# Rows of x by indexed gathers on GpSimd in place of plain loads on ScalarE's queue

## The chip, the cores and the metric

The kernel runs on one NeuronCore of one Trainium2 chip. The metric is the device time of one execution in microseconds (us). Engines are called PE (TensorE, with PEld for its weight loads), DVE (VectorE), ACT (ScalarE), POOL (GpSimd) and SP (SyncE). ACTq and SPq are the sequencers of ACT and SP, which issue transfers. L235 is line 235 of a kernel. All runs quoted are fast, which here means that none was more than 1.5% above the fastest of its kernel. The granted clock is the share of its full clock that PE was allowed.

A ratio below is the mean time of one kernel's fast runs over the mean of the other's fast runs in the same rounds, so it isn't quite the ratio of the medians that are quoted beside it. Brackets behind a ratio are its 95% interval.

## The reference, cut to what matters

Four graph layers over 2708 nodes with 512 features each follow one another, each with a residual and a layer norm. All of them multiply by the same 2708 x 2708 adjacency. Layer 0, and the counts that layer 1 needs, are:

```python
adj_hat = adj + eye(N)
d = 1.0 / sqrt(adj_hat.sum(axis=1))
x = layernorm(x + (d[:, None] * adj_hat * d[None, :] @ x) @ W.T + b)   # layer 0
mask = adj > 0           # layer 1 divides by roots of the row counts of this mask
# layers 1 to 3: further products with adj, attention, binarized weights (left out)
```

## The kernel before

The change touches the first stage only. It goes over 22 blocks of 128 rows (the last has 20). For each block it loads the rows of x and a row tile of the adjacency, computes x times W0 on PE, sums the adjacency rows on ACT, counts their non-zeros on DVE, and takes the power -1/2 of each sum on GpSimd. Layer 0 can start its first product when all blocks of `fc` are there.

```python
nc.scalar.dma_start(b0_row, over_partitions(b0, D))    # then bg_row, ba_col, bb_col, all on ACT's queue
...
weights(w0, w0_t)                                      # 1 MB, on ACT's queue too
for b in range(NB):
    m = rows(b)
    nc.scalar.dma_start(fb[b][:m], x[b * P : b * P + m, :])                 # L235
    ar = pre.tile([P, N], F32, tag="arow", name=f"arow{b}", bufs=2)         # two buffers
    nc.sync.dma_start(ar[:m], adj[b * P : b * P + m, :])                    # L237, 1.39 MB
    xt = transposed(pre, fb[b], b, F32, ident, "xt0_")                      # PE (L187), copied by ACT (L189)
    ps = project(xt, b, w0, "y0_")                                          # PE, 8 products for two blocks (L196)
    nc.scalar.activation(ar[:m], ar[:m], AF.Copy, accum_out=row_sum[:m, b : b + 1])   # L240, the "sum"
    nc.vector.tensor_scalar(ar[:m], ar[:m], 0.0, 0.0, op0=ALU.is_gt, op1=ALU.add,
                            accum_out=row_cnt[:m, b : b + 1])               # L241, the "count"
    dc = dinv[:m, b : b + 1]
    nc.vector.tensor_scalar(dc, row_sum[:m, b : b + 1], 1.0, None, op0=ALU.add)
    nc.gpsimd.tensor_tensor(dc, dc, neg_half[:m], op=ALU.pow)               # L247
    nc.vector.tensor_scalar(fc[b][:m], ps[:m], dc, None, op0=ALU.mult)      # L248
    nc.vector.tensor_tensor(fb[b][:m], fb[b][:m], b0_row[:m], op=ALU.add)   # L249, the bias add
```

SP's queue also carries chunks of the transposed adjacency for layer 0, seven of them in the first 64 us. A scheduler orders the instructions of each engine, and one that waits holds up those behind it: in the kernel before, ACT had summed adjacency tile 0 by 12.2 us, but DVE's count of it, behind a bias add that waited for x until 21.97 us, started at 22.57. An edit to one line can move the others.

Of the kernel before, what the change touches and what calls it, by code (L numbers as in the profile page):

```python
# [12 lines left out]
PSUM = bass.MemoryType.PSUM  # L13

P = 128
# [5 lines left out]


def over_partitions(row: bass.AP, n: int):
    """A contiguous row of n elements in DRAM, read once per partition."""
    return bass.AP(tensor=row.tensor, offset=row.offset, ap=[[0, P], [1, n]])


# [1 line left out]
def kernel(  # L29
# [15 lines left out]
    w3_t: bass.AP,  # L45
    out: bass.AP,
):
    """Four residual graph layers with layer norm.

    Every product with the adjacency takes 128 x 128 tiles of its transpose (contraction index on  # L50
    the partitions) as the stationary operand and 128 x 512 node features as the moving one. The
    features stay in SBUF in three buffers of one tile per 128 nodes; the transposed adjacency, which
    doesn't fit beside them, is streamed in column groups, ahead of the products.
    """
    nc = tc.nc
    N, D = x.shape
    KC = D // P
    NB = -(-N // P)
    W = 2 * P
# [3 lines left out]
    AHEAD = 6  # L63
    PREP = 2
# [7 lines left out]
    def blocks(g: int):  # L72
        return [b for b in (2 * g, 2 * g + 1) if b < NB]

    # The contraction tiles of one column group, in chunks of one load each: (first tile, tiles, rows).
    parts = [(j, min(CH, NFULL - j), P) for j in range(0, NFULL, CH)]
    if N % P:
        parts.append((NFULL, 1, N % P))
# [5 lines left out]
    stream = ctx.enter_context(tc.tile_pool(name="stream", bufs=AHEAD + 1))  # L84
# [5 lines left out]
    fa = [feat.tile([P, D], F32, tag=f"fa{b}", name=f"fa{b}") for b in range(NB)]  # L90
    fb = [feat.tile([P, D], F32, tag=f"fb{b}", name=f"fb{b}") for b in range(NB)]
    fc = [feat.tile([P, D], F32, tag=f"fc{b}", name=f"fc{b}") for b in range(NB)]
# [5 lines left out]
    ones = const.tile([P, 1], F32, name="ones")  # L98
# [11 lines left out]
    bb_col = const.tile([P, 1], F32, name="bb_col")  # L110
    nc.scalar.dma_start(bb_col, over_partitions(bb, 1))

    # Per node, node b * 128 + p at [p, b]; the rows that the last block lacks stay 1.
    row_sum = const.tile([P, NB], F32, name="row_sum")
    row_cnt = const.tile([P, NB], F32, name="row_cnt")
    dinv = const.tile([P, NB], F32, name="dinv")
    head = const.tile([P, NB], F32, name="head")
    rdeg = const.tile([P, NB], F32, name="rdeg")
    nc.vector.memset(row_sum, 1.0)
    nc.vector.memset(row_cnt, 1.0)  # L120
    # x3 columns: x.Wa[:D], x.Wa[D:], x.Wb[:D], x.Wb[D:], h.a[:D], h.a[D:]
    cols = const.tile([P, NB, 6], F32, name="cols")
    nc.vector.memset(cols, 1.0)

# [1 line left out]
    chunk_of = {}  # L126
    issued = [0]

# [14 lines left out]
            issued[0] += 1  # L143

    def run_layer(layer: int, products, prep, finish):
        """products names a block's PSUM accumulators; prep(g, part, adj) gives, for each of them, what
        a chunk's products read: (stationary chunk, moving tiles); finish(b, *accumulators) ends a
        block. prep runs PREP chunks ahead of the products, the loads AHEAD."""
        base = layer * PER_LAYER
        ready = {}  # L150
        acc = {}
        for k in range(PER_LAYER):
            for q in range(k, min(k + PREP, PER_LAYER - 1) + 1):
                if q not in ready:
                    load_until(base + q + (AHEAD - PREP))
                    ready[q] = prep(*divmod(q, NPART), chunk_of.pop(base + q))
            g, part = divmod(k, NPART)
            operands = ready.pop(k)
            if part == 0:
                acc = {  # L160
                    b: [ps_mm.tile([P, D], F32, tag="mm", name=f"l{layer}_{n}_{b}") for n in products]
                    for b in blocks(g)
                }
            j0, nj, r = parts[part]
            for jj in range(nj):
                j = j0 + jj
                for ib, b in enumerate(blocks(g)):
                    m = rows(b)
                    for ps, (lhs, rhs) in zip(acc[b], operands):
                        nc.tensor.matmul(  # L170
                            ps[:m, :],
                            lhs[:r, jj, ib * P : ib * P + m],
                            rhs[j][:r, :],
                            start=(j == 0),
                            stop=(j == NB - 1),
                        )
            if part == NPART - 1:
                for b in blocks(g):
                    finish(b, *acc[b])

# [1 line left out]
    def transposed(pool, src, b: int, dt, eye, name: str):  # L182
        """Rows of block b with the features on the partitions: [128, D / 128, rows]."""
        m = rows(b)
        ps = ps_sm.tile([P, KC, P], dt, tag="sm", name=f"{name}p{b}")
        for k in range(KC):
            nc.tensor.transpose(ps[:, k, :m], src[:m, k * P : (k + 1) * P], eye[:m, :m])  # L187
        t = pool.tile([P, KC, P], dt, tag=name, name=f"{name}{b}", bufs=2)
        nc.scalar.copy(t[:, :, :m], ps[:, :, :m])  # L189
        return t  # L190
# [8 lines left out]
        return ps  # L199

    def as_row(dst, src, name: str):
        """dst[:, i] = the value of node i on every partition; src(b) is block b's column."""
        for b0_ in range(0, NB, KC):
            ps = ps_sm.tile([P, KC * P], F32, tag="sm", name=f"{name}{b0_}")
            n = 0
            for b in range(b0_, min(b0_ + KC, NB)):
                m = rows(b)
                nc.tensor.transpose(
                    ps[:, n : n + m], src(b)[:m].to_broadcast([m, P]), ident[:m, :m]
                )  # L210
                n += m
            nc.scalar.copy(dst[:, b0_ * P : b0_ * P + n], ps[:, :n])
# [13 lines left out]
    def weights(dst, src):  # L226
        nc.scalar.dma_start(dst, src.rearrange("(k p) o -> p k o", p=P))

# [1 line left out]
    with tc.tile_pool(name="pre0", bufs=1) as pre:  # L230
        w0 = pre.tile([P, KC, D], F32, name="w0")
        weights(w0, w0_t)
        for b in range(NB):
            m = rows(b)
            nc.scalar.dma_start(fb[b][:m], x[b * P : b * P + m, :])  # L235
            ar = pre.tile([P, N], F32, tag="arow", name=f"arow{b}", bufs=2)
            nc.sync.dma_start(ar[:m], adj[b * P : b * P + m, :])  # L237
            xt = transposed(pre, fb[b], b, F32, ident, "xt0_")
            ps = project(xt, b, w0, "y0_")
            nc.scalar.activation(ar[:m], ar[:m], AF.Copy, accum_out=row_sum[:m, b : b + 1])  # L240
            nc.vector.tensor_scalar(  # L241
                ar[:m], ar[:m], 0.0, 0.0, op0=ALU.is_gt, op1=ALU.add,
                accum_out=row_cnt[:m, b : b + 1],
# [5 lines that stand above are left out]
            nc.vector.tensor_tensor(fb[b][:m], fb[b][:m], b0_row[:m], op=ALU.add)  # L249
        nc.gpsimd.tensor_tensor(head, row_cnt, half, op=ALU.pow)  # L250
        nc.vector.tensor_scalar(head, head, HEAD_EPS, None, op0=ALU.max)
        nc.vector.reciprocal(head, head)
        nc.vector.tensor_tensor(rdeg, row_cnt, head, op=ALU.mult)
        nc.vector.tensor_tensor(rdeg, rdeg, row_sum, op=ALU.add)
        nc.vector.reciprocal(rdeg, rdeg)

# [1 line left out]
    def finish0(b, ps):  # L258
        m = rows(b)
        t = work.tile([P, D], F32, tag="t", name=f"t0_{b}")  # L260
# [5 lines left out]

    run_layer(0, ["y"], lambda g, part, a: [(a, fc)], finish0)

# [1 line left out]
    with tc.tile_pool(name="l1", bufs=1) as l1:  # L270
        head_row = l1.tile([P, N], F32, name="head_row")
        as_row(head_row, lambda b: head[:, b : b + 1], "head_")
# [20 lines left out]

        run_layer(1, ["e"], prep1, finish1)

# [1 line left out]
    with tc.tile_pool(name="l2", bufs=1) as l2:  # L297
        sl_row = l2.tile([P, N], F32, name="sl_row")
        with tc.tile_pool(name="pre2", bufs=1) as pre:
# [34 lines left out]
            nc.vector.tensor_scalar(cols[:, :, 1], cols[:, :, 1], ba_col, None, op0=ALU.add)  # L334
            nc.vector.tensor_scalar(cols[:, :, 3], cols[:, :, 3], bb_col, None, op0=ALU.add)

# [1 line left out]
        # The attention's columns of adj, and sum e, are summed over the contraction tiles on  # L338
        # VectorE and GpSimd, and over the partitions by one product with ones for each block.
        with tc.tile_pool(name="main2", bufs=2) as main:  # L340
            sums = {}

# [65 lines left out]

            run_layer(2, ["b", "a"], prep2, finish2)

# [1 line left out]
    with tc.tile_pool(name="pre3", bufs=1) as pre:  # L412
        w3 = pre.tile([P, KC, D], F32, name="w3")
        weights(w3, w3_t)
# [9 lines left out]
            ps = project(xt, b, bw, "xw_")  # L424
            nc.vector.tensor_copy(fc[b][:m], ps[:m])

# [1 line left out]
    def finish3(b, ps):  # L428
        m = rows(b)
        t = work.tile([P, D], F32, tag="t", name=f"t3_{b}")  # L430
# [50 lines left out]
```

## Time and profile before

| | before |
|---|---|
| median of 2 runs | 2584.46 us (2584.16 to 2584.76) |
| PE busy before layer 0's first product, 0 to 152.6 us | 102.86 us |
| PE busy in layer 0, 152.6 to 584 us | 429.22 of 431.40 us |
| ACT's sum of adjacency tile 6 starts | 63.53 us |
| ACT's sum of adjacency tile 20 starts | 144.64 us |
| issues of x on ACT's queue | 22, median 0.416 us |

Where PE is full (429.22 of 431.40 us), nothing that the change does can matter. The first 152.6 us are read by three landmarks: the sum of tile 6 (end of a disturbed start), the sum of tile 20 (end of a regular loop), and layer 0's first product. The group of the x loads shows why they are worth a look at all. Its first line gives count, shortest, median and longest issue in ns, and the start of the first and last. Below it stands who waited for them, in us and times:

```profile
L235 ACTq DMA_DIRECT2D fb<-in_x_dram x22: 334/416/621, 3.6 to 64.0; - x22
...
who waited for it (us, times):
  PE xt_p L187: 20.8, 1
```

PE waited once, 20.8 us, for the first of them.

### The profile page before, as it was taken

Reading aid. Unit: us, or ns where it says so; the run is one execution under the profiler, and the core shown is the slowest. Engines: PE = TensorE matmul, PEld = TensorE weight load, DVE = VectorE, ACT = ScalarE, POOL = GpSimd, SP = SyncE. Lnnn points to the kernel's source line nnn. Section 1 sums busy time; section 2 is a strip of 40 time slices with the busy share of each in tenths; the row PEclk is TensorE's granted clock in tenths of the full one; section 3 lists DMA queues with packets and bytes.
Section 4 is the critical chain, followed back from the end, with each engine's and each line's share of the span. In section 5 each row is a group of like instructions: output and inputs, shape, how many; then the busy total and the mean of one; then the engine's idle time right before and its main releaser. Section 6 shows DMA issues by size and latency. Waiting matters only on the chain.

```text
span 2585.0 us, 16339 instructions
## 1 busy us (share of the span) xinstructions
PE 2486.2 (96%) x6073; PEld 1065.1 (41%) x6073; DVE 996.6 (39%) x1771; ACT 342.0 (13%) x560; POOL 273.5 (11%) x359
## 2 busy tenths in 40 slices
PE   5799999999999998999999999999999989999998
PEld 2334444424444442444444444444444324444442
DVE  4731110115444542001866656676656332011011
ACT  3510000000000000111323222232212211000000
POOL 0010000000000000000322212222222100000000
PEclk9899999999999998999999999999999989999999
DMA  8632222222222222000111111111111011223220
GB/s 320 225 106 68 72 76 69 68 61 80 71 71 80 68 54 73 0 1 0 31 31 37 31 43 32 34 35 37 37 32 26 23 47 52 81 85 90 82 83 27
DMA packets 136625, 164.07 MB, mean 63 GB/s; under 512 B 6822, under 2 KB 125990, under 8 KB 133838
## 3 DMA queue, kind: packets, MB, share of 16 engines
q1 hardware_dynamic: 127574, 146.69, 19.9%
q10 hardware_dynamic: 8972, 16.35, 1.8%
q8 instruction: 47, 0.77, 0.1%
q14 instruction: 32, 0.26, 0.0%
HBM read 157.46 MB, written 5.55 MB: 63 GB/s over the span
## 4 chain that ended last, share of the span: by engine, by line
PE 94%; DMA 3%; DVE 1%; ACT 1%; issue 1%; ACTq 0%; POOL 0%; POOLq 0%; DVEq 0%
PE l_b L170 17%; PE l_e L170 17%; PE l_a L170 16%; PE l_o L170 16%; PE l_y L170 16%; PE h L196 3%; PE g L196 3%; PE y L196 2%; DMA arow<-in_adj_dram 1%; DMA fb<-in_x_dram 1%; PE xw L196 1%; ACT xt L189 1%; PE xt_p L187 1%; PE ps L386 1%; PE pc L327 1%
## 5 line engine op out<-in xcount | busy, mean ns | idle before, releaser
L170 PE MATMUL l_b<-fc,adj 128*128 128x512 f32 x968 | 511.1, 610 | 0.0
L170 PE MATMUL l_a<-fa,e 128*128 128x512 f32 x968 | 504.3, 604 | 0.0
L170 PE MATMUL l_e<-fa,inc 128*128 128x512 f32 x968 | 427.8, 599 | 2.1 <-DVE inc L283 2.1
L170 PE MATMUL l_y<-fc,adj 128*128 128x512 f32 x968 | 426.1, 597 | 0.0
L170 PE MATMUL l_o<-fc,adj 128*128 128x512 f32 x968 | 426.1, 597 | 0.0
L170 PEld LDWEIGHTS l_a<-fa,e 128*128 128x128 f32 x968 | 183.8, 190 | 244.0 <-issue 239.9
L170 PEld LDWEIGHTS l_b<-fc,adj 128*128 128x128 f32 x968 | 178.6, 190 | 246.7 <-issue 244.7
L170 PEld LDWEIGHTS l_e<-fa,inc 128*128 128x128 f32 x968 | 175.1, 186 | 254.0 <-issue 243.4
L170 PEld LDWEIGHTS l_y<-fc,adj 128*128 128x128 f32 x968 | 174.5, 185 | 251.5 <-issue 243.8
L170 PEld LDWEIGHTS l_o<-fc,adj 128*128 128x128 f32 x968 | 174.5, 185 | 251.1 <-issue 244.3
L374 POOL TENSOR_TENSOR sum_e<-sum_e,e 128x256 f32<-128x256 f32 (+2 forms) x231 | 186.3, 806 | 470.6 <-ACT e L364 458.5
L221 POOL TENSOR_TENSOR rs<-rs,neg_half 128x1 f32<-128x1 f32 x88 | 64.1, 729 | 1378.0 <-DVE rs L220 1242.5
L376 DVE SCALAR_TENSOR_TENSOR sum_a<-adj,cols,sum_a 128x256 f32<-128x256 f32 (+2 forms) x231 | 141.3, 612 | 44.8 <-DMA adj<-in_adj_t_dram 44.8
L431 DVE SCALAR_TENSOR_TENSOR t<-l_o,fb 128x512 f32<-128x512 f32 (+1 forms) x22 | 15.0, 682 | 370.5 <-PE l_o L170 370.5
L280 DVE SCALAR_TENSOR_TENSOR inc<-adj,head_row 128x768 f32<-128x768 f32 (+1 forms) x88 | 75.3, 857 | 213.0 <-PE l_e L170 212.3
L376 DVE SCALAR_TENSOR_TENSOR sum_b<-adj,cols,sum_b 128x256 f32<-128x256 f32 (+2 forms) x231 | 152.2, 659 | 0.0
L261 DVE TENSOR_TENSOR t<-l_y,fc 128x512 f32<-128x512 f32 (+1 forms) x22 | 15.1, 687 | 350.1 <-PE l_y L170 350.1
L364 ACT ACTIVATE e<-e 128x768 f32<-128x768 f32 (+1 forms) x88 | 67.5, 767 | 528.0 <-DVE e L363 527.7
L362 DVE TENSOR_SCALAR e<-adj 128x768 f32<-128x768 f32 (+1 forms) x88 | 46.3, 526 | 229.9 <-PE l_a L170 229.7
L196 PE MATMUL y<-w,xt 128*128 128x512 f32 (+1 forms) x176 | 92.7, 686 | 28.9 <-ACT xt L189 28.9
L189 ACT COPY xt<-xt_p 128x512 f32<-128x512 f32 (+1 forms) x66 | 35.4, 566 | 566.2 <-PE xt_p L187 558.2
L355 ACT ACTIVATE z<-sl_row,cols 128x256 f32<-128x256 f32 (+1 forms) x242 | 103.0, 485 | 0.0
(94 smaller groups left out, 1268.6 us busy)
## 6 DMA issues: line engine op xcount, KB each, us to landing
adj<-in_adj_t_dram SPq DMA_DIRECT2D x280, 384.0 KB
arow<-in_adj_dram SPq DMA_DIRECT2D x21, 1354.0 KB
adj<-in_adj_t_dram SPq DMA_DIRECT2D x28, 222.0 KB
fb<-in_x_dram ACTq DMA_DIRECT2D x21, 256.0 KB
out_dram<-o ACTq DMA_DIRECT2D x21, 256.0 KB
w<-in_w_t_dram ACTq DMA_DIRECT2D x2, 1024.0 KB
wsa<-in_w_sa_dram ACTq DMA_DIRECT2D x1, 1024.0 KB
wg<-in_w_gcnb_dram ACTq DMA_DIRECT2D x1, 1024.0 KB
```

The lines of the kernel that those rows point to most:

```text
L170: nc.tensor.matmul(ps[:m, :], lhs[:r, jj, ib * P : ib * P + m], rhs[j][:r, :], start=(j == 0), stop=(j == NB - 1),)
L187: nc.tensor.transpose(ps[:, k, :m], src[:m, k * P : (k + 1) * P], eye[:m, :m])
L189: nc.scalar.copy(t[:, :, :m], ps[:, :, :m])
L196: nc.tensor.matmul(ps[:m, :], xt[:, k, :m], weight[:, k, :], start=(k == 0), stop=(k == KC - 1))
L221: nc.gpsimd.tensor_tensor(rs[:m], rs[:m], neg_half[:m], op=ALU.pow)
L280: nc.vector.scalar_tensor_tensor(inc[:r, :nj, :w], av, 0.0, row, op0=ALU.is_gt, op1=ALU.mult)
L327: nc.tensor.matmul(pc[:m, :6], xt[:, k, :m], vec[:, :, k], start=(k == 0), stop=(k == KC - 1))
L355: nc.scalar.activation(z[:r, jj, :w], sl_row[:r, g * W : g * W + w], AF.Identity, bias=cols[:r, j0 + jj, 5:6],)
L362: nc.vector.tensor_scalar(ev, av, 0.0, MASKED, op0=ALU.is_equal, op1=ALU.mult)
L364: nc.scalar.activation(ev, ev, AF.Exp, scale=-1.0)
L374: nc.gpsimd.tensor_tensor(se[:r, :w], se[:r, :w], ej, op=ALU.add)
L376: nc.vector.scalar_tensor_tensor(s[:r, :w], aj, u, s[:r, :w], op0=ALU.mult, op1=ALU.add)
```

## The change

Its intent is to take 22 load issues off ACT, which also does the sums and the copies. GpSimd was busy for 12.98 of the first 152.6 us. A column of row numbers is made once, and each block of x is fetched by an indexed gather whose indices are just its own row numbers. The diff also blanks comments and docstrings, which is cut here:

```diff
@@ -226,13 +226,20 @@
     with tc.tile_pool(name="pre0", bufs=1) as pre:
+        node = pre.tile([P, NB], mybir.dt.int32, name="node")
+        nc.gpsimd.iota(node, pattern=[[P, NB]], base=0, channel_multiplier=1)
         w0 = pre.tile([P, KC, D], F32, name="w0")
         weights(w0, w0_t)
         for b in range(NB):
             m = rows(b)
-            nc.scalar.dma_start(fb[b][:m], x[b * P : b * P + m, :])
+            nc.gpsimd.indirect_dma_start(
+                out=fb[b][:m],
+                out_offset=None,
+                in_=x,
+                in_offset=bass.IndirectOffsetOnAxis(ap=node[:m, b : b + 1], axis=0),
+            )
```

## The prediction

> **What bounds the kernel now.** I read the page first, then the execution cut into its stages, then the chain of waits of the first stage in order of time, then that stage's timeline.
>
> The page's chain that ended last says that nearly all of the span is TensorE:
>
> ```profile
> PE 94%; DMA 3%; DVE 1%; ACT 1%; issue 1%; ACTq 0%; POOL 0%; POOLq 0%; DVEq 0%
> PE l_b L170 17%; PE l_e L170 17%; PE l_a L170 16%; PE l_o L170 16%; PE l_y L170 16%; PE h L196 3%; PE g L196 3%; PE y L196 2%; DMA arow<-in_adj_dram 1%; DMA fb<-in_x_dram 1%; PE xw L196 1%; ACT xt L189 1%; PE xt_p L187 1%; PE ps L386 1%; PE pc L327 1%
> ```
>
> The change touches only "DMA fb<-in_x_dram 1%". The execution by stage (columns: stretch in us, its length, busy us of PE, weight loads, DVE, ACT, POOL with counts, granted clock, DMA share, GB/s):
>
> ```profile
> 0.00:152.60 152.60, 102.86 (x265) 46.92 (x265) 94.18 (x114) 67.74 (x67) 12.98 (x27) 0.92 0.71 257
> 152.60:584.00 431.40, 429.22 (x991) 176.84 (x990) 63.81 (x141) 2.92 (x6) 15.88 (x23) 1.00 0.25 68
> ```
>
> From 152.6 us on PE is full (429.22 of 431.40), and no x is read any more. So the change can act on the first 152.6 us alone, 6% of 2584.46. There no engine is full; DMA share is 0.71. The chain of waits of that stage (start us, us, what):
>
> ```profile
> 3.58 17.13 DMA fb<-in_x_dram
> 20.84 1.10 PE xt_p L187 x4
> ...
> 113.12 8.83 PE y L196 x16
> 121.95 0.89 PE xt_p L187 x8
> 122.87 0.90 issue
> 123.77 0.20 ACT arow L240
> 123.99 2.98 DVE arow L241 x2
> 126.97 0.03 DVE dinv L246
> 127.00 6.16 DMA arow<-in_adj_dram
> ```
>
> Two regimes. At the start everything waits for the first x tile, which lands at 20.7 us. From about 60 us on it is a loop: DVE counts an adjacency row tile (2.98), its buffer (one of two) comes free, the next tile is loaded (6.16; others 5.6 to 5.7), ACT sums it (2.46 + 0.19), DVE counts it. 5.7 + 2.65 + 2.97, plus small gaps, makes about 11.4 us for a buffer, two tiles. The trace agrees: ACT's sum of tile 6 starts at 63.53, of tile 20 at 144.64, 14 tiles in 81.1 us, 5.79 us each. The x tiles were all asked for by 64.05 us and are not in that loop.
>
> The start in the timeline:
>
> ```profile
> 12.04 0.19 ACT L240 ACTIVATION_READ_ACCUMULATOR arow<-arow 128x1 f32 x1
> ...
> 21.97 0.69 DVE L249 TENSOR_TENSOR fb<-fb,b_row 128x512 f32<-128x512 f32 x1 [20.40 <-PE xt_p L187]
> ...
> 22.57 2.96 DVE L241 TENSOR_SCALAR_CACHE_REDUCE arow<-arow 128x2708 f32<-128x2708 f32 x1
> ...
> 25.58 3.29 SPq L237 DMA_DIRECT2D arow<-in_adj_dram  x2
> ```
>
> Tile 0 was summed at 12.2 us, but its count on DVE stands behind the bias add of x tile 0, so it started at 22.57, and the third adjacency load was issued only at 25.58. DMA is loose there: 170 GB/s from 20 to 25 us against 344 to 404 from 30 to 50.
>
> [...] the early stretches at 344 to 404 GB/s look like a shared limit. [...] ACT's issues took 334 to 621 ns (median 416) here; the trace has no gather. [...]
>
> **The change part by part.** I compared the built orders of both kernels.
>
> *Removed from ACT*: 22 issues of about 0.42 us, 9.2 us in all. ACT is busy 67.74 of 152.6 us and waits 59.8 us for adjacency tiles, so this alone is worth nothing; what matters is that ACT's later x loads stood behind its sums and copies.
>
> *Added on GpSimd*: one iota (128 x 22) and 22 gathers. Before, GpSimd is busy 12.98 us here. [...] Eight semaphores serve the gathers, so the ninth and later ones each wait for the landing of the one eight before. GpSimd also computes the powers that release DVE's scaling of each block, and in the new order the power of block 2 stands behind gather 19 and that of block 3 behind gather 21, the last. After that GpSimd is as before.
>
> *Moved on DVE and SP*: the count of adjacency tile 0 now comes before the first bias add. It can start when ACT has summed tile 0: 12.2 us before, perhaps 13 now as three queues share the start. Then the third adjacency load goes out near 16 us in place of 25.6, 9 us earlier.
>
> *How much of the 9 us is kept.* The early stage then runs into DMA. Before the sum of tile 6 can start, 7 tiles of 1.39 MB (9.7 MB), 7 transposed chunks of 0.39 MB (2.75), W0 and two bias rows (1.57) and most of x (14 to 22 tiles of 0.26, 3.7 to 5.8 MB) must move: 17.7 to 19.8 MB. Before, about 20 MB had moved by 63.5 us (296, 296 and 347 GB/s over three 20 us stretches, then 361). With fewer holes at 340 to 360 GB/s from 2.5 us on, that is 52 to 60 us; I take 57.5, so 6 us gained.
>
> *The loop* has the same cycle; only the pairing of blocks shifts by one (0-1, 2-3 in place of 0, 1-2, 3-4). From tile 6 on I expect 5.7 to 5.8 us a tile, no gain.
>
> *The tail*: before, block 21 stood alone after the sum of tile 20, and its product started at 147.36, 1.9 us of PE idle, then layer 0 at 152.6. Now blocks 20 and 21 are a pair ahead of the sum of tile 20, so layer 0 may start about 2 us sooner.
>
> Sum: 6 + 2 = 8 us. 2584.5 - 8 = 2576.5; I say 2577.
>
> **Rivals.** (1) *GpSimd becomes the gate.* If a gather holds it for g us, the power of block 3 comes at about 2 + 22g us. The count of tile 4 comes some 3 us after it (scalings 2 x 0.75, two bias adds 1.3), and it started at 51.97 before. So it equals the kernel before at g = (51.97 - 5)/22 = 2.1 us; each further us costs 22. At g = 3 the kernel takes about 20 us more, 2604; over 2% slower (52 us) needs g of about 4.5. For it: in-order GpSimd, and no measured gather. [...] The same gate through landings: gather 21 waits for gather 13, which at a quarter to a third of 350 GB/s lands near 35 to 45 us. That fits, but narrowly.
> (2) *x pushes ahead of adjacency.* Up to eight gathers in flight, 2.1 MB, are 6 us at 350 GB/s; if they only delay tiles 0 to 3 and leave no hole filled, the gain is gone: 2584 to 2588.
> (3) *The first x was the whole trouble*: without that wait all 9 to 10 us plus the tail are kept, 2572.
> (4) *Hidden anyway*: 2584.
>
> **Range and chances.** Rivals 2 to 4 lie between 2572 and 2588, a slow gather of up to 2.4 us adds about 6 to the upper end. I take 2566 to 2591. To be 2% faster the first stage would have to shrink from 152.6 to 101 us, under its 102.86 us of PE work: 1%. 2% slower needs gathers over 4 us each: 2%. Within: 97%.
>
> **What would show it.** Right: DVE's first count near 13 to 16 us, the third adjacency load before 18, layer 0's first product near 145, and every later stage within 1 us. ACT's sum of tile 6 near 57 shows the DMA step; 5.7 to 5.8 us a tile after it shows the loop unchanged. Wrong: DVE's scalings waiting many us for the powers of blocks 2 and 3 (rival 1, and the gathers' own durations give g); tiles 0 and 1 landing well after 10 and 20 us (rival 2); a longer loop period, or a change after layer 0 began, which I hold for impossible.

## The result and the profile after

The changed kernel takes 2579.09 us (median of 2 runs, 2578.07 to 2580.10). The ratio is 0.9989 [0.9969, 1.0009]: within 2%, and 5.4 us lower by the medians. The profiled spans are 2576.3 and 2585.0 us.

The page's chain that ended last, of the changed kernel:

```profile
PE 94%; DMA 3%; issue 1%; DVE 1%; ACT 1%; ACTq 0%; POOL 0%; POOLq 0%; SPq 0%; DVEq 0%
PE l_b L170 17%; PE l_e L170 17%; PE l_o L170 16%; PE l_y L170 16%; PE l_a L170 16%; PE h L196 3%; PE g L196 3%; PE y L196 2%; DMA arow<-in_adj_dram 1%; DMA w<-in_w_t_dram 1%; PE xw L196 1%; ACT xt L189 1%; PE ps L393 1%; PE pc L334 1%; PE xt_p L187 1%
```

It is the same chain, except that the 1% of waiting for x has become 1% of waiting for W0. By stage (stretch, its length, then busy us of PE, weight loads, DVE, ACT and POOL with counts, granted clock, DMA share, GB/s):

```profile
0.00:146.20 146.20, 103.19 (x265) 47.60 (x265) 92.06 (x112) 65.84 (x66) 33.97 (x49) 0.89 0.74 269
146.20:584.00 437.80, 436.52 (x1005) 180.76 (x1005) 71.64 (x153) 4.81 (x8) 17.56 (x25) 1.00 0.26 68
```

The first stage is 6.4 us shorter with the same PE work. From the start of layer 0's first product to the start of its last it is 425.5 us in both kernels (152.6 to 578.1 before, 146.2 to 571.7 after). Everything from layer 0's first product to the end took 2432.4 us before and 2430.1 after. Over the profiles of all kernels that remainder lies anywhere from 2426.4 to 2434.9, so it tells nothing, and the first stage is what is compared.

The start, in the timeline of the changed kernel (start, us, engine, line, what):

```profile
0.97 0.15 POOL L232 IOTA node<- 128x22 int32 x1
...
8.31 0.94 POOL L237 DMA_INDIRECT fb<-in_x_dram,node  x1 [0.30 <-issue]
...
12.89 2.97 DVE L248 TENSOR_SCALAR_CACHE_REDUCE arow<-arow 128x2708 f32<-128x2708 f32 x1 [11.27 <-ACT arow L247]
...
15.90 0.34 SPq L244 DMA_DIRECT2D arow<-in_adj_dram  x1
```

The count of tile 0 starts at 12.89 us (22.57 before) and the third adjacency load goes out at 15.90 (25.58 before). Of these 9.7 us, 5.2 are left when that tile can be summed (28.74 us against 33.94): it took 12.8 us to land, 8.4 before, at a DMA share of 0.99 to 1.04 from 2.5 to 44.4 us. Also, x itself is early now: PE's first transposes, which wait for the first x tile, start at 10.60 us (20.84 before). The 22 gathers as a group, and what GpSimd waited for ahead of them:

```profile
L237 POOL DMA_INDIRECT fb<-in_x_dram,node x22: 895/956/1205, 1.8 to 38.1; - x22
its engine sat idle before it (us, times) until:
  issue: 5.4, 19
  DMA fb<-in_x_dram,node: 1.5, 2
```

A gather holds GpSimd for 0.956 us, and consecutive ones start 1.26 us apart. Only two waited for an earlier one to land. Where more of the gain was lost shows in the products of x with W0, one line for each pair of blocks:

```profile
22.16 9.66 PE L196 MATMUL y<-w,xt 128*128 128x512 f32 x16 [7.46 <-DMA w<-in_w_t_dram]
...
32.99 7.13 PE L196 MATMUL y<-w,xt 128*128 128x512 f32 x16 [0.29 <-ACT xt L189]
...
48.89 9.96 PE L196 MATMUL y<-w,xt 128*128 128x512 f32 x16 [7.89 <-ACT xt L189]
```

The third pair came after a wait of 7.89 us and took 9.96 us where the second took 7.13. The granted clock of PE in that stretch, first the changed kernel, then one with plain loads on GpSimd's queue (described below) where PE had no such wait:

```profile
44.00:54.00 10.00, 5.11 (x6) 2.17 (x7) 3.05 (x3) 5.96 (x6) 0.55 (x1) 0.52 0.72 253
```

```profile
44.00:54.00 10.00, 8.49 (x26) 3.93 (x25) 6.34 (x8) 6.05 (x6) 0.93 (x1) 1.00 0.82 298
```

The clock was 0.52 in the one and 1.00 in the other. In the changed kernel's trace the records of the clock begin at 27.31 us and it changes at 44.38, 54.62 and 78.51 us: 1.00 for 17.07 us, 0.50 for 10.24 and 1.00 for 23.89, which are 5, 3 and 7 times 3.41 us. Cut into windows of that length, the changed kernel shows (second figure after the stretch: busy us of PE; third from the end: clock):

```profile
40.97:44.38 3.41, 0.03 (x1) 0.00 (x0) 1.96 (x3) 0.00 (x0) 0.14 (x1) 1.00 1.02 411
...
47.79:51.21 3.42, 2.32 (x3) 1.17 (x4) 2.81 (x1) 3.42 (x5) 0.00 (x0) 0.50 0.61 196
51.21:54.62 3.41, 3.41 (x5) 1.33 (x4) 0.23 (x3) 0.56 (x2) 0.55 (x1) 0.50 0.63 200
54.62:58.03 3.41, 3.41 (x9) 1.52 (x8) 2.50 (x2) 0.00 (x0) 0.00 (x0) 1.00 0.49 206
```

A window with 0.03 us of PE work was followed by half clock (0.50). In the window in which the pair began PE was busy for 2.32 us, and half clock lasted through the next, full one (3.41 us): 5.7 us of products in all. Waits of 8.33 us in a second profile of this kernel and of 6.13 us before the pair at 66.61 us in the kernel before were followed by a clock of 0.50 too.

That pair matters because of ACT's order: the sum of tile 6 stands behind the copy of block 6's transposes, and these stand behind the pair on PE:

```profile
59.38 0.58 ACT L189 COPY xt<-xt_p 128x512 f32<-128x512 f32 x1 [7.61 <-PE xt_p L187]
59.86 2.46 ACT L247 ACTIVATE arow<-arow 128x2708 f32<-128x2708 f32 x1
```

### The profile page after: what moved, and what is told of

It reads as the page before. It is cut to its first block, busy times and chain, and to the rows that moved or that the text cites. A ratio compares the mean times of both kernels' runs of the same rounds, so it can differ in the third digit from the quotient of the medians.

```text
span 2576.3 us, 16349 instructions
## 1 busy us (share of the span) xinstructions
PE 2483.8 (96%) x6070; PEld 1065.4 (41%) x6073; DVE 997.3 (39%) x1771; ACT 342.0 (13%) x560; POOL 293.8 (11%) x382
## 4 chain that ended last, share of the span: by engine, by line
PE 94%; DMA 3%; issue 1%; DVE 1%; ACT 1%; ACTq 0%; POOL 0%; POOLq 0%; SPq 0%; DVEq 0%
PE l_b L170 17%; PE l_e L170 17%; PE l_o L170 16%; PE l_y L170 16%; PE l_a L170 16%; PE h L196 3%; PE g L196 3%; PE y L196 2%; DMA arow<-in_adj_dram 1%; DMA w<-in_w_t_dram 1%; PE xw L196 1%; ACT xt L189 1%; PE ps L393 1%; PE pc L334 1%; PE xt_p L187 1%
```

## The experiments

My theory after the result had four parts. The gain comes from DVE's order (the count of tile 0 no longer behind x), not from ACT's freed queue and not from indexing. The start is then held back by full DMA and by the late W0. GpSimd doesn't gate anything at 0.96 us a gather. The loop is set by its own chain of waits. The rivals are named with each run; the second run corrects the first part. This table holds the landmarks of all profiles (us):

| kernel | median | ratio to before | sum of tile 6 | a tile in the loop | sum of tile 20 | layer 0 |
|---|---|---|---|---|---|---|
| before | 2584.46 | 1 | 63.53 | 5.79 | 144.64 | 152.6 |
| after | 2579.09 | 0.9989 | 59.86 | 5.76 | 140.52 | 146.2 |
| after, again | 2578.30 | 0.9991 | 58.72 | 5.77 | 139.49 | 144.1 |
| plain loads, GpSimd's queue | 2578.58 | 0.9985 | 56.37 | 5.80 | 137.63 | 143.9 |
| plain loads, SP's queue | 2559.23 | 0.9912 | 50.95 | 6.05 | 135.60 | 125.2 |
| GpSimd made slow | 2599.89 | 1.0065 | 78.68 | 5.72 | 158.81 | 166.0 |
| one bias add moved | 2578.07 | 0.9982 | 57.15 | 5.78 | 138.02 | 144.3 |
| after, W0 first | 2574.16 | 0.9971 | 56.30 | 5.72 | 136.41 | 141.5 |
| SP's queue, W0 first | 2554.54 | 0.9887 | 47.14 | 6.00 | 131.10 | 119.9 |
| after, half tiles | 2556.55 | 0.9893 | 46.32 | 4.61 | 110.79 | 125.9 |
| before, half tiles | 2562.83 | 0.9931 | 46.67 | 4.81 | 113.97 | 133.1 |
| after, half tiles, W0 first | 2555.97 | 0.9907 | 45.83 | 4.61 | 110.39 | 125.5 |
| SP's queue, half tiles, W0 first | 2552.68 | 0.9888 | 39.10 | 5.13 | 110.98 | 120.9 |
| after, sum of tile 6 first | 2586.94 | 1.0011 | 57.07 | 6.10 | 142.46 | 154.4 |

"A tile" is the difference of the two sums' starts over 14. The kernel before had medians of 2581.76 to 2582.75 us beside these runs. All kernels were correct. Each row is one profile; that of the kernel before is of a run some 2 us above those medians, so one or two us against its landmarks are not certain.

**The changed kernel again.** No edit, 5 rounds.

> The changed kernel itself, repeated to measure its gain more closely than two runs do. My theory (the gain is made in the first stage: 3.7 us by the sum of tile 6, 0.4 in the loop, 2.3 in the tail, as the two profiles show): 5 to 8 us below the kernel before, so a ratio of 0.997 to 0.998, and layer 0's first product again near 146 us against 152.6. The rival (no gain, two lucky runs): a ratio within 0.9995 to 1.0005, or layer 0 starting above 151 us.

It took 2578.30 us (2575.63 to 2582.45), 0.9991 [0.9977, 1.0004]. The interval just includes no gain, but the profile repeats the first one: the wait before the third pair was 8.33 us, the clock 0.50 from 43 to 52 us, layer 0 at 144.1.

**Plain loads on GpSimd's queue.** This drops the indices alone.

```diff
-            nc.scalar.dma_start(fb[b][:m], x[b * P : b * P + m, :])
+            nc.gpsimd.dma_start(fb[b][:m], x[b * P : b * P + m, :])
```

> x by plain loads from GpSimd's queue, no indices. By the built order the pairing of blocks is that of the kernel before (0, 1-2, 3-4, block 21 alone), so this is the queue without the indices and without the new tail. My theory (queue and order give the start's gain, the pairing gives the tail's): half of the gain stays, 3 to 5 us below before, about 2580.5, with the tail from the sum of tile 20 to layer 0 back at 7.5 to 8 us. Rival A (the indices cost something): faster than the changed kernel, 2575 or less. Rival B (the queue alone is everything and the tail is noise): the same as the changed kernel within 1 us.

The time was 2578.58 us, 0.9985 [0.9971, 0.9999], the same as with gathers. An issue took 0.538 us in place of 0.956. So indexing neither costs nor brings anything that shows; moving the loads does it all. I had expected half of the gain; what came is rival B's time. And DVE's order is the old one here:

```profile
10.87 0.69 DVE L249 TENSOR_TENSOR fb<-fb,b_row 128x512 f32<-128x512 f32 x1 [8.16 <-PE xt_p L187]
...
12.87 2.97 DVE L241 TENSOR_SCALAR_CACHE_REDUCE arow<-arow 128x2708 f32<-128x2708 f32 x1 [1.31 <-ACT arow L240]
```

The bias add still stands ahead of the count of tile 0, but x tile 0 is there early, the bias add is done before ACT has summed tile 0, and the count starts when that sum releases it, as in the changed kernel. So a new order on DVE is not needed; an early x does the same. In this kernel block 21 is still a block of its own behind the sum of tile 20, as before, and layer 0 was nonetheless at 143.9. The tail of 7.5 to 8 us that I expected was 6.3. Pairing is therefore not needed for that date.

**Plain loads on SP's queue.** This tests whether GpSimd matters at all.

```diff
-            nc.scalar.dma_start(fb[b][:m], x[b * P : b * P + m, :])
+            nc.sync.dma_start(fb[b][:m], x[b * P : b * P + m, :])
```

> x by plain loads on SP's queue in line with the adjacency tiles; GpSimd issues nothing, ACT issues nothing. Here x is paced by the adjacency buffers, and the transposed chunks come late. My theory (in the changed kernel x and the chunks fill DMA until about 48 us and leave it idle after, so x ahead of need costs start time): the sum of tile 6 starts near 50 to 55 us in place of 59.9, and the kernel takes 2570 to 2576. Rival (sharing one queue puts 0.26 MB, about 0.7 us, into each turn of the loop): 0.7 x 22 = 15 us longer than that, 2585 to 2592, with the period of a tile at 6.3 us or more in place of 5.76.

It took 2559.23 us, 0.9912 [0.9898, 0.9925], more than expected. The sum of tile 6 was inside the expected range, and the loop was slower by 0.26 us a tile. I put that down to x and adjacency sharing a queue, which no run tests. What I had missed is the order that the scheduler made of it. It puts the copies of the transposes up to four blocks ahead of the sums on ACT, so PE is busy for 92.97 of the 105.51 us from 19.69 us, when W0 is there, to 125.2, and layer 0 starts before the sums of the last tiles are done.

**GpSimd made slow.** A useless power of 128 x 8 elements beside each gather, about 1.7 us.

```diff
+        junk = pre.tile([P, 8], F32, name="junk")
 ...
+            nc.gpsimd.tensor_tensor(junk, half[:, :8], half[:, :8], op=ALU.pow)
```

> The changed kernel with one useless power of 128 x 8 on GpSimd beside each gather, so GpSimd's time a gather rises and no byte more moves. From the 3.86 us of the 128 x 22 power I estimate 1.4 to 1.7 us each, so 2.7 to 3.0 us a gather in place of the 1.26 us of spacing measured. The first rival of the prediction as a formula: the power of block 3 comes at about 2 + 22 x 2.85 = 65 us, the count of tile 4 some 3 us later, in place of 48.4: 18 us longer than the changed kernel, 2592 to 2602. If GpSimd's place in line gates nothing: 2577 to 2582.

The time was 2599.89 us, 1.0065 [1.005, 1.0081], as rival (1) of the prediction reckoned. Gathers were some 2.9 us apart. In the list of waits (total us, times, longest), the changed kernel first, then this one:

```profile
DVE fc L255 <- POOL dinv L254: 11.1, 17, 0.7
```

```profile
DVE fc L257 <- POOL dinv L256: 39.9, 19, 21.9
```

DVE waited at most 0.7 us for a power with gathers alone, and 21.9 us once with the slow GpSimd. The count of tile 4 moved from 48.40 to 69.97 us. The gate is real, and gathers of 0.96 us don't reach it.

**DVE's order alone.** The kernel before with block 0's bias add on GpSimd; x stays on ACT's queue with all its 22 issues.

```diff
-            nc.vector.tensor_tensor(fb[b][:m], fb[b][:m], b0_row[:m], op=ALU.add)
+            bias = nc.gpsimd if b == 0 else nc.vector
+            bias.tensor_tensor(fb[b][:m], fb[b][:m], b0_row[:m], op=ALU.add)
```

> The kernel before, with the bias add of block 0 alone moved from DVE to GpSimd, so that DVE's count of adjacency tile 0 no longer stands behind the landing of x tile 0; x is loaded as before, on ACT's queue. Theory A (the gain comes from DVE's order: the count of tile 0 early, so the third adjacency load early): count of tile 0 near 13 us, third adjacency load near 16 us, ACT's sum of tile 6 at 59 to 61 us, layer 0's first product at 147 to 150, 3 to 5 us faster than before. Rival (the early x on another queue is what helps): tile 6 at 62 us or later, 0 to 2 us faster.

The time was 2578.07 us, 0.9982 [0.9968, 0.9996], all that the change gives. Its timeline:

```profile
12.11 2.97 DVE L241 TENSOR_SCALAR_CACHE_REDUCE arow<-arow 128x2708 f32<-128x2708 f32 x1 [10.54 <-ACT arow L240]
19.60 8.66 SPq L237 DMA_DIRECT2D arow<-in_adj_dram  x2
21.90 1.26 POOL L250 TENSOR_TENSOR fb<-fb,b_row 128x512 f32<-128x512 f32 x1 [20.59 <-PE xt_p L187]
```

The count of tile 0 is early, although x tile 0 still comes late (the bias add, now on GpSimd, waits for it until 21.90). The third adjacency load went out at 19.60, later than the 16 expected, and yet tile 6 (57.15) and layer 0 (144.3) came earlier than expected. The gain does not need ACT's queue freed, nor an early x. Moving one bias add out of the way on DVE is enough. Nor did the later third load show: the sum of tile 2 started at 30.20 us here, against 28.74 in the changed kernel and 31.67 with plain loads on GpSimd's queue, where that load went out at 15.9.

**W0 first.** The changed kernel with the four small loads put behind W0 on ACT's queue.

```diff
-    nc.scalar.dma_start(b0_row, over_partitions(b0, D))     # and bg_row, ba_col, bb_col
 ...
         weights(w0, w0_t)
+        nc.scalar.dma_start(b0_row, over_partitions(b0, D)) # and the other three
```

> The changed kernel with the load of W0 put first on ACT's queue, ahead of the bias rows, which follow it. Theory A (what limits the gain now is DMA that is full until about 48 us): W0 lands near 10 us in place of 22, the first product of x with W0 near 12 us, but ACT's sum of tile 6 moves by no more than 1.5 us (58 to 60) and the time by no more than 1.5 us. Rival C (the late W0 is the gate of the start, since PE works at its limit until the loop of adjacency tiles has caught up): tile 6 at 52 to 56 us, 4 to 8 us faster than the changed kernel.

The time was 2574.16 us, 0.9971 [0.9957, 0.9985]. W0 landed at 17.7 us, not at 10. The sum of tile 6 moved to 56.30 and layer 0 to 141.5. That lies outside what I expected if DMA alone was the limit (58 to 60) and just short of the rival's range for tile 6 (52 to 56). So the late W0 held part of the start. The third pair still came after a wait (6.76 us) and at half clock (0.50 from 44 to 50 us; the pair took 9.11 us), so this is a term beside that one. The interval overlaps the changed kernel's, so the 4 us by the medians are likely, not certain.

**SP's queue and W0 first.** The two edits together.

> Plain loads of x on SP's queue, and the load of W0 first on ACT's queue. With plain loads on SP's queue alone, PE was busy almost without a hole from the landing of W0 at 19.7 us to layer 0 at 125.3. Theory C (there the first stage is bound by PE, started late by W0): W0 lands near 10 us, layer 0 starts 7 to 10 us earlier, 115 to 119 us, and the time is 2549 to 2553. Rival (bound by the landing of adjacency tiles): layer 0 starts within 3 us of 125 and the time stays near 2559.

The time was 2554.54 us, 0.9887 [0.9871, 0.9902]; layer 0 at 119.9, 5.3 us earlier than without W0 first. The first product moved only from 19.69 to 15.10 us, less than expected, and layer 0 followed it. PE was busy for 93.47 of the 104.80 us from 15.10 to 119.90: nearly, not wholly, bound by PE.

**Half tiles, after.** Each adjacency row tile is loaded, summed and counted as two column halves in four buffers, with the same bytes and the same memory.

```diff
-            ar = pre.tile([P, N], F32, tag="arow", name=f"arow{b}", bufs=2)
-            nc.sync.dma_start(ar[:m], adj[b * P : b * P + m, :])
+            for h in range(2):
+                ar = pre.tile([P, N // 2], F32, tag="arow", name=f"arow{b}_{h}", bufs=4)
+                nc.sync.dma_start(ar[:m], adj[b * P : b * P + m, h * (N // 2) : (h + 1) * (N // 2)])
 ...             # sum and count of each half into sum2, cnt2; added up for dinv and at the end
```

> The changed kernel with each adjacency row tile loaded, summed and counted as two column halves in four buffers of half the size, partial sums added afterwards: the same bytes and the same SBUF. The loop of before is load, sum and count of a whole tile in turn in each of two buffers, 5.8 us a tile. Theory A (that chain of waits sets the pace of the loop, not DMA, which is at a share of 0.7): 4.9 to 5.3 us a tile between tiles 6 and 20, layer 0's first product at 133 to 139, time 2565 to 2573. Rival (DMA or PE sets the pace): 5.6 to 5.8 us a tile, time 2577 to 2581.

The time was 2556.55 us, 0.9893 [0.9877, 0.9909], more than expected. A tile took 4.61 us, against 5.76. Half-tile sums cost more on ACT (the median in ns is the middle of three):

```profile
L257 ACT ACTIVATE arow<-arow x44: 1315/1333/1347, 8.3 to 115.8; 128x1354 f32<-128x1354 f32 x42, 20x1354 f32<-20x1354 f32 x2
```

Two sums of 1.33 us replace one of 2.46, and still the loop is faster. Its pace was thus set by the chain of load, sum and count in each of two buffers, not by DMA or by ACT's work. The DMA share rose to 0.90 before layer 0 (0.74 in the changed kernel).

**Half tiles, before.** The same edit on the kernel before, to see what the change is worth on a faster loop.

> The kernel before (x on ACT's queue) with each adjacency row tile handled as two column halves in four buffers, so the change is now tried on a loop that is faster: the changed kernel with halves had 4.6 us a tile, layer 0 at 125.9 us, and 0.9893 of the time before. Theory A (the change moves the start, and its gain is kept whatever the loop does): counts of tile 0 behind the bias add of block 0 at 21 to 23 us, layer 0 at 130 to 134, time 2561 to 2567, that is 4 to 8 us over the changed kernel with halves. Rival (in the faster loop with four buffers the late start is made up, or the change costs something there): layer 0 at 123 to 128, time 2553 to 2559.

The time was 2562.83 us, 0.9931 [0.9918, 0.9944], and layer 0 at 133.1. It is 7.2 us later than in the changed kernel with half tiles. The size is as expected, but its place isn't: the sum of tile 6 was equal (46.67 against 46.32). The loop lost 0.2 us a tile, 2.8 us in 14, and the last 4.0 us came after the sum of tile 20. I had also expected both counts of tile 0 behind the bias add; the first half was counted at 9.88 us, only the second stood behind it (21.08). As for the 6.8 us lost after tile 6, two of the last four pairs of products, at 95.02 and 115.92 us, took 8.83 us in place of 7.13, and the granted clock was 0.95 from 21.1 to 133.1 us; in the changed kernel with half tiles all pairs from 91.69 us on took 7.13 to 7.24, and the clock was 0.99 up to layer 0. That is up to 3.4 us; the rest I haven't looked for.

**Half tiles, after, W0 first.**

> The changed kernel with halves and with the load of W0 ahead of the bias rows. W0 first alone landed W0 at 17.7 in place of 22 us and gave the changed kernel some 4 us. Theory C (the late W0 is a gate of the start): layer 0 at 121 to 124 in place of 125.9, time 2551 to 2555. Rival (with halves the adjacency loop alone sets the time): layer 0 at 125 to 127, time 2555 to 2559.

The time was 2555.97 us, 0.9907 [0.9892, 0.9922]: no gain over half tiles alone. W0, though first on its queue, landed only at about 21 us (the first product that reads it started at 21.18), so this run doesn't settle what an early W0 would bring there.

**Half tiles, SP's queue, W0 first.**

> Halves, plain loads of x on SP's queue, W0 first: all that has helped, together. With x on SP's queue and W0 first the first stage had layer 0 at 119.9. Theory C (PE is the bound of that kernel's first stage, some 105 us of work from about 12 us on): halves add little, layer 0 at 116 to 120, time 2550 to 2555. Rival (adjacency tiles still limit it): layer 0 at 108 to 115, time 2541 to 2549. If it is slower than 2556, x behind more and smaller adjacency loads on one queue costs more than it brings.

The time was 2552.68 us, 0.9888 [0.9873, 0.9903], the lowest median and no better by ratio than SP's queue with W0 first alone. DMA share was 0.93 at 324 GB/s from 13.78 us to layer 0, and PE was busy for 91.18 of those 107.12 us. Which of the two is the limit there stays open.

**The sum of tile 6 first.** Four useless products in PE's wait before the third pair make the scheduler put ACT's sum of tile 6 ahead of the copy for block 6. An edit that filled the whole wait, to see whether the clock then stays at 1.00, would have reordered more, so it was not run.

```diff
+            if b == 3:
+                warm = ps_mm.tile([P, D], F32, tag="mm", name="warm")
+                for _ in range(4):
+                    nc.tensor.matmul(warm, ident, w0[:, 0, :], start=True, stop=True)
```

> The changed kernel with four useless products of 0.44 us in a wait of PE of 7.9 us; they are there because the scheduler then puts ACT's sum of tile 6 ahead of the copy of block 6's transposes, where the changed kernel has it behind. The third pair of products stays behind the sum of tile 4, and the wait before it stays over 6 us. Theory D (in the changed kernel tile 6 had landed and its sum stood behind the third pair, which ran at half clock after PE's wait: 9.96 us in place of 7.13): the third pair again takes 9 to 10 us at a granted clock of 0.5, but ACT's sum of tile 6 starts at 56.9 to 57.9 in place of 59.86, by the landing of the tile. Rival (the landing of tile 6 set it, DMA): 59 us or later. The same edit puts the pair of blocks 20 and 21 behind the sum of tile 20. If the pairing at the end is worth anything, layer 0 then starts some 10 to 11 us after that sum starts, in place of 4.6 to 5.7, at 147 to 150, and the time is 2579 to 2584; if it is worth nothing, layer 0 starts at 142 to 145.

PE's third pair, and ACT's sum of tile 6:

```profile
48.77 9.74 PE L196 MATMUL y<-w,xt 128*128 128x512 f32 x16 [4.70 <-ACT xt L189]
...
57.07 2.46 ACT L251 ACTIVATE arow<-arow 128x2708 f32<-128x2708 f32 x1 [5.42 <-DMA arow<-in_adj_dram]
```

The pair was as slow as before (9.74 us, the clock at 0.50 from 48 to 54 us), after a wait of 4.70 us. I had expected over 6, but the four useless products took 3.60 us, 0.90 each and not 0.44. And the sum started at 57.07 us, released by the landing of its tile. In the changed kernel the tile is asked for at nearly the same time (51.41 against 51.28 us), and its sum started 2.8 us later. So the pair ahead of it, and not the landing, is what held it there. The time, 2586.94 us, 1.0011 [0.9994, 1.0027], missed its range. The loop was slower as well (6.10 us a tile); I put that down to the new order, and had not foreseen it. The end of the stage, first before, then the changed kernel, then this one:

```profile
147.36 5.31 PE L196 MATMUL y<-w,xt 128*20 128x512 f32 x8 [1.86 <-ACT xt L189]
152.60 7.99 PE L170 MATMUL l_y<-fc,adj 128*128 128x512 f32 x18
```

```profile
139.03 7.24 PE L196 MATMUL y<-w,xt 128*128 128x512 f32 x16 [1.01 <-ACT xt L189]
146.20 14.00 PE L170 MATMUL l_y<-fc,adj 128*128 128x512 f32 x32
```

```profile
145.53 8.94 PE L196 MATMUL y<-w,xt 128*128 128x512 f32 x16 [3.61 <-ACT xt L189]
154.40 11.00 PE L170 MATMUL l_y<-fc,adj 128*128 128x512 f32 x25
```

From the start of the sum of tile 20 to layer 0 it is 8.0 us before, 5.7 after (4.6 in its second profile), 6.3 in both kernels that keep block 21 alone with an early count of tile 0, and 11.9 here, where the whole pair stands behind that sum.

## Why the prediction was right or wrong

The time (2579.09 against 2577.0), the range and the class held. The gain is smaller than the 7.5 us that this meant: 5.4 us by the first medians, 3.9 by those of five runs, and the interval of both ratios includes no gain. The steps:

*The start: right mechanism, mis-sized.* The count of tile 0 and the third adjacency load came when predicted. That the late count was what cost the kernel before its start is shown from two sides: with the count put ahead and x still late (one bias add moved), and with the old order and x early (plain loads on GpSimd's queue). The changed kernel has both; the new order that I named is enough, but it was not needed. I predicted -6 us at the sum of tile 6 (57.5); it was -3.7 (59.86), and -4.8 in the second profile. The step that failed is the reading that the sum of tile 6 would come as soon as DMA had moved its 17.7 to 19.8 MB. The landing of the tile did come at that date, 57.07 us where the order let it show. The term that I left out is PE's clock: the pair of products ahead took 9.96 us at half clock in place of 7.13 (9.18 in the second profile), up to 2.8 us against a miss of 2.4. That it would have been 57.0 us at full clock is worked out, not run. The kernel before had shown it: its pairs took 7.13 us at full clock, and 10.14 us after the wait of 6.13 us. I read waits of PE as free as long as PE was no bound. They weren't here, where ACT's order hung on the products after them. W0 is a second term that I left out: it came at 22 us and became what PE's first products waited for; having it first brought 2.4 to 3.6 us at tile 6 (56.30 against 58.72 and 59.86).

*ACT's issues "worth nothing": right.* A kernel that keeps them had the same time. What I added, that it mattered that later x loads stood behind ACT's sums and copies, the same run does not bear out: there they still stand behind them.

*GpSimd: right.* That it would not become the gate was my estimate, and no trace that I had then showed a gather, so this was partly luck. Measured, a gather takes 0.956 us and consecutive ones start 1.26 us apart, below the 2.1 us that rival (1) reckoned for g. That sum was right too: slowed on purpose to some 2.9 us, GpSimd gated as it says.

*The loop: right.* 5.76 us a tile against 5.79. The half tiles show that its chain of waits is what sets it.

*The tail: right size, largely by luck.* It was -2.3 us against -2. The pairing ahead of the last sum explains 0.6 us (1.6 in the second profile): 5.7 and 4.6 against 6.3. The other 1.7 us is that before, block 21's eight products ran at half clock: 5.31 us against 3.61 in both kernels that keep that block alone. In the kernel before, the wait ahead of them (1.86 us) lay within one window of 3.41 us, from 144.38 to 147.79 us, in which PE was busy for 1.55 us; the clock was 0.50 in the next. With plain loads on GpSimd's queue PE had waited as long ahead of them (2.02 us) and kept the full clock (1.00 from 134 to 158 us); counted from its change at 60.61 us, a window ended at 139.1, inside that wait. The windows fell elsewhere from run to run (the clock first fell to 0.50 at 44.38 us in one profile of the changed kernel and between 42 and 43 in the other). That these 1.7 us hang on where they fell in the one profile of the kernel before is my reading; no run tests it, and none shows that the change brings them.

*"Every later stage within 1 us": not to be checked so.* Layer 0's products agree within 0.1 us, but the whole remainder varies by 8.5 us between profiles of different kernels.

*Rivals.* (2) did not come: the sum of tile 1 started at 14.00 us, against 22.45 before. (The second figure is no landing: that sum stood behind a copy which waited for x. The sign named for (2), tile 1 landing well after 20 us, did not show.) (3) did not come, and not for the half clock alone: the runs without that slow pair, plain loads on GpSimd's queue and one bias add moved, kept 7.2 and 6.4 us at tile 6, not 9 to 10. The landmarks speak against (4), and so do the intervals of those two runs (up to 0.9999 and 0.9996); that of the changed kernel itself includes it.

## What to carry to other kernels

Look first for the one instruction that stands in front of another on its engine; moving it, or letting what it waits for come earlier, can be worth as much as moving a whole stream of transfers (here 0.9982 and 0.9989). When a wait of PE of several us lies ahead of products that something else stands behind, look at the clock of those products too (here pairs of 7.13 us took 8.83 to 10.14 after waits of 2.38 to 8.33 us, though not after every such wait). And where a faster version is wanted, look at what the chain of buffers, the queue and the scheduler's order make of it: finer tiles, or plain loads on SP's queue, gave 0.989 and 0.991 here, the change itself 0.999.

## What the runs show of issues, queues and the clock

- A gather of 128 rows of 2 KB held GpSimd for 0.956 us (0.895 to 1.205) with 0.30 us between gathers; the issue of a plain load took 0.538 us on GpSimd and 0.416 us on ACT's queue.
- In this kernel the same plain loads gave 2582.18 us on ACT's queue, 2578.58 on GpSimd's and 2559.23 on SP's, with other work behind the issues and another order made by the scheduler.
- In the first 165 us of the profiles of the kernel before and of the changed kernel every change of clock lies on a grid of 3.41 us. Nine windows at full clock in which PE was busy for 0.00 to 1.31 us were followed by half clock (0.50), those with 1.70 us or more were not; of two between, the one with 1.55 was and the one with 1.42 wasn't. At half clock six windows with 0.00 to 2.68 us were followed by half clock, ten with 3.02 us or more by full clock. (Ends of products are modelled in these traces, so the busy times are rough.) Later in both profiles windows with PE busy for all 3.41 us were followed by half clock too (at 1304.91 us before, at 1297.07 after), so these figures hold for this stage alone. In two more runs: an idle time of 2.4 us that lay mostly in one window (57.20 to 60.61 us with plain loads on GpSimd's queue, PE busy for 1.17 us) was followed by a clock of 0.50, and one of 3.7 us split between two (1.64 and 1.51 us busy, half tiles with W0 first) was not.
- Gathers beside DVE's counts took 0.95 to 1.00 us (17.16 to 19.72 us), those without a count beside them 0.94 to 0.95 (3.31 to 8.31 us).
